# Where the outputs of a recurrent layer are computed: in the scans' slots or in the attention's gaps

## The chip, the core and the metric

The kernel runs on one core of a Trainium2 chip. The metric is the device time of one execution in microseconds: 1647.23 us is the median of three runs (1642.21 to 1647.71). Its engines are TensorE (PE in the profile; PEld is its loading of weights), VectorE (DVE), ScalarE (ACT), GpSimd (POOL) and SyncE (SP, which here only issues DMAs). SBUF is the memory on the chip that all of them work from, PSUM the one that TensorE writes to.

## What is computed

Eight batches of 512 tokens with 256 features go through four layers, each added to its input after a layernorm. All is fp32.

```python
x = x + _L0_attn_a_ref(_layernorm(x), ...)   # a: layernorm, Mamba mixer with a scan over the tokens, FFN 256-1024-256
x = x + _L0_ffn_ref(_layernorm(x), ...)      # b: a recurrence over the batches, then an output
x = x + _L0_attn_b_ref(_layernorm(x), ...)   # c: attention, 16 heads of 16 features
x = x + _L0_ffn_ref(_layernorm(x), ...)      # d: the same recurrence as b, same weights

# b and d: x is [8, 512, 256]; the recurrence runs over the 8 batches, all tokens side by side
def step(c, xt):
    ft = sigmoid(xt @ wf.T + c @ uf.T + bf)
    it = sigmoid(xt @ wi.T + c @ ui.T + bi)
    gt = tanh(xt @ wc.T + c @ uc.T + bc)
    return ft * c + it * gt
h = tanh(x @ wo.T + c_final @ uo.T + bo)     # every batch's output needs the state behind the last batch
```

So the output of layer b has two parts: a product x @ wo of each batch by itself, and a product of the final state, one for all batches, which is known only when the recurrence has gone through all eight.

## The kernel before

The work goes in three stages. The order of the instructions on PE, DVE and ACT is written out by hand, as short words in strings that name pieces of work; the order of POOL and SP is written out too in the first stage, and behind it is left to a scheduler.

**Stage 1, Mamba and recurrence b** (`mamba_and_recurrence`, L847). A batch's scan takes 16 slots, a line of text each (SLOTS, L789; LAST, L809, for the last batch; REST, L828, for what stands behind the last scan). Each slot scans two units of eight channels (`scan_pair`, L420: the scan at L424 and a product at L428, both on DVE), whose inputs SP loads from DRAM. In the slots stand pieces of other batches: of the next one its preparation (`i`, `e`), of the previous one the Mamba output and the FFN (`o`: projection L464, `up` L518, `down` L542), and recurrence b. Recurrence b of a batch begins in the next batch's slots (`r`) and ends in those of the one behind (`q`). `recurrent_step` (L615) makes its pieces: stats, norm, transposes (`turn`), and for each gate (f, i, g) and half m of the features a product with the inputs (`gate_inputs`, L595), one with the state (`gate_state`, L604) and a tanh (L610); `hold` and `update` (L677, L686, L687) make the new state on DVE. The pieces `output0` and `output1` (L691 to L702) multiply the transposed input by wo, a half of the tokens each, 8 matmul instructions of 128x256 in the profile; `output_` copies the sum from PSUM to SBUF (L707), and behind the second half the tile `pre` is stored to DRAM by a DMA that ACT issues (L710).

**Stage 2, attention c and recurrence d** (`attention`, L1239). A batch has 4 groups of 4 heads, and a group 4 rows of 128 tokens, which makes 16 rows. In each row the program goes: the scores of the next group for its maxima (`row_max`, L1084; PE at L1079 to the PSUM tag `two` with three buffers, DVE maximum L1090), the first gap of GAPS (L1191), the scores for the exponents (`attend`, L1109; the same tag, ACT exponent L1116), the second gap. The word `v` in a gap (`catch_up`, L1284) is the values' product of the row before (L1125), and in the rows 4, 8, 12 and 0 it ends a group: `collect` (L1134) copies the group's sum out on ACT (L1141) and SP issues eight DMAs of 32 KB, four to `o_c` and four to `sum_c` (L1146). `max` is the transposition of the maxima and their sum into the queries (L1101, L1106). The other words are pieces: `n` the preparation of the next batch, `d` and `e` recurrence d of the batch two behind and one behind, so that attention batches 0 and 1 have none of `d`; `c` and `o` the division by the sums (`divide{k}{half}`, L1155: reciprocal L1158 and product L1160 on DVE; k = 0 needs groups 0 and 1, k = 1 groups 2 and 3) and the output projection (L1166). Apart from `two`, gaps' products share one PSUM buffer, tag `one`.

The words `p` are what is left of layer b's output (`late_output`, L1211): load `pre` back from DRAM (L1218, one buffer), add the state's part `cu` (L1222), tanh (L1225), add to x (L1229). Batches 0 and 1 are done ahead of the rows, batches 2 to 7 in the gaps of attention batches 0 to 5, one each.

**Stage 3** (`stage_d_rest`, L1307) ends recurrence d and writes the outputs.

The function `part_of` (L119) gives the first half (".a"), the second (".b") or all of the tokens; `recurrent_step` and the FFN's pieces take such a half, and a gate of half the tokens keeps its PSUM in the tag `da` and its scratch in the scan's buffers (`hc`, L668 to L671).

Of the kernel before, what the change touches and what calls it, by code (L numbers as in the profile page):

```python
# [15 lines left out]
P = 128  # L16
B = 8
L = 512
# [596 lines left out]
def recurrent_step(cx, d, b, tok, tok_tag, ch, ch_tag, t=None, half=None):  # L615
# [27 lines left out]

    def turn_(k):
        nc.scalar.copy(t.xT[:, k, tk], ps_of["turn", k][:, tk])
        if k == KC - 1 and d.keep:
            d.xT[b] = cx.xdram.tile([P, KC, L], F32, tag=f"xT{b}", name=f"xT_dram_{n}")
            nc.sync.dma_start(d.xT[b], t.xT)

    def inputs(g, m):  # L650
        ps_of[g, m] = gate_inputs(cx, n, g, m, t.xT, fill(), tk)
# [27 lines left out]
    def update(m):  # L679
# [8 lines left out]
        if m == KC - 1 and half != 0:  # L688
            d.s = t.s

    def output(i):  # L691

        ps_of["output", i] = ps = cx.psum.tile([P, 2, E], F32, tag=fill(), name=f"ps_o_{n}_{i}")
        for j in range(2):
            for k in range(KC):
                nc.tensor.matmul(
                    ps[:, j, :],
                    t.xT[:, k, ts(2 * i + j, P)],
                    cx.gw[:, WO, k, :],
                    start=(k == 0),  # L700
                    stop=(k == KC - 1),
                )  # L702
# [10 lines left out]
    for name, f in (  # L713
        ("turn{}", turn), ("turn{}_", turn_), ("hold{}", hold), ("update{}", update),
        ("output{}", output), ("output{}_", output_),
    ):
        for i in range(2):
            pieces[name.format(i)] = lambda f=f, i=i: f(i)
    for g in range(3):
        for m in range(KC):  # L720
            for what, f in (("", product), ("_", tanh), ("x", inputs), ("s", state), ("s_", tanh)):
# [104 lines left out]
""".strip().split("\n")  # L826

REST = """  # L828
y o.gate1 o.proj0 o.proj1 o.add_proj o.stats o.norm o.residual
o.turn0 o.turn0_ o.turn1 o.turn1_ o.up0 o.up0_ o.up1 o.up1_ o.up2 o.up2_ o.up3 o.up3_ o.down0  # L830
o.down1 o.add0 o.up4 o.up4_ o.up5 o.up5_ o.add1 o.up6 o.up6_ o.up7 o.up7_ o.down2 o.down3 o.add2
o.add3 r.stats r.norm r.turn0 r.turn0_ r.turn1 r.turn1_
r.f0 r.f0_ r.hold0 r.i0 r.i0_ r.g0 r.g0_ r.update0
r.f1 r.f1_ r.hold1 r.i1 r.i1_ r.output0 r.output0_ r.g1 r.g1_ r.update1 r.output1 r.output1_
""".strip().split("\n")

FRONT = """
# [9 lines left out]
def mamba_and_recurrence(cx, a, w, d):  # L847
# [3 lines left out]
    for b, t in enumerate(T):  # L851
        t.da, t.hc, t.bx, t.dl_rep, t.dx_rep, t.y, t.ps = {}, {}, {}, {}, {}, {}, {}
        i = mamba_in(cx, a, t, b)
        o = mamba_out(cx, a, t, b)
        r, shared = {}, Ctx()
        for half in (None,):
            r |= recurrent_step(cx, d, b, cx.tok, "h", cx.ch, ("T", 3), shared, half)
        for who, ahead, pieces in (
            ("e", 2, i), ("i", 1, i), ("a", 0, i), ("c", 0, o), ("o", -1, o), ("r", -1, r), ("q", -2, r),
        ):  # L860
            parts[who, b - ahead] = pieces

    def piece(b, one):
        who, what = one.split(".", 1)
        if (who, b) in parts:
            parts[who, b][what]()

    for one in FRONT.split():
# [320 lines left out]


GAPS = """  # L1191
d.turn0 v n.stats d.turn1 | d.f0x
v | -
v o.divide10 | d.f0s
v d.i0x d.i0s n.norm | max
v | o.divide11 o.project0
n.turn0 | p.load v
d.g0x d.g0s | v
v n.turn1 | n.queries0 max
v | p.sum o.project1  # L1200
d.update0 d.f1x e.stats | v
v d.f1s | n.vals1 n.queries1 p.tanh
v | max
d.i1x d.i1s c.divide01 | v
n.vals0 | c.divide00 v
v p.add e.norm | d.g1x
d.g1s d.update1 | max v
""".strip().split("\n")


def late_output(cx, cu, d, b):  # L1211

    nc = cx.nc
    t = Ctx()

    def load():
        t.pre = cx.att.tile([P, TC, E], F32, tag="pre", bufs=1, name=f"pre_back_{b}")
# [21 lines left out]
def attention(cx, c, d, d_b, cu):  # L1239
# [19 lines left out]
        for b in range(B)  # L1259
    }  # L1260
    for b in range(2, B):
        parts["p", b - 2] = late[b]
    for b in range(B):
        parts["n", b - 1] = attention_in(cx, c, b)
        parts["c", b] = parts["o", b + 1] = attention_out(cx, c, b)
# [24 lines left out]
    for at, (b, g) in enumerate(steps):  # L1290
        po = None
        for t in range(TC):
            if at + 1 < len(steps):
                b1, g1 = steps[at + 1]
                row_max(cx, c, b1, c.made[b1], g1, t)
            first_gap, second_gap = GAPS[g * TC + t].split("|")
            fill(b, g, first_gap)
            es = attend(cx, b, c.made[b], g, t)
            fill(b, g, second_gap)
# [207 lines left out]
```

## Time and profile before

| | |
|---|---|
| median of 3 runs | 1647.23 us |
| profiled execution | 1647.11 us, its span 1645.3 us |
| mean granted TensorE clock | 0.949 |
| scans, one batch, from the third on | some 86 us |
| from the last scan's gate to the first attention scores (749.98 to 849.84) | 99.9 us |
| attention batch 0, 1, a later one (first scores to first scores) | 77.5, 75.9, 92.0 us |
| output products of layer b (L696) | 128 matmul instructions, 0.215 us apart when nothing waits |
| load of pre (L1218), 8 of 512 KB | 3.2 to 3.6 us from issue to landing |

How to read it: the page gives busy time by engine; stretches give the same between two times, with the clock granted to TensorE; the timeline lists instructions in order of time, runs of one kind merged, with start, length, engine, line, output<-inputs and shape; brackets name what ended an idle time. The chain of waits is followed back from the last instruction to what released each step. A matmul's end is modelled, so its start and the next one's start say more than its length.

### The profile page before, as it was taken

How to read it: one execution, taken by the hardware profiler on the slowest of the kernel's cores; microseconds unless marked ns; L12 is line 12 of the kernel's file. 1: busy time of each engine (PE TensorE's matmuls, PEld its weight loads, DVE VectorE, ACT ScalarE, POOL GpSimd, SP SyncE). 2: the span in 40 equal slices, each digit the busy share in tenths (PEclk: the TensorE clock that was granted, in tenths of full speed). 3: DMA queues.
4: the chain of work that ended last, by engine and by line, in shares of the span. 5: the costliest groups of instructions: out<-in, count | busy, mean ns of one | idle time of the engine just before them, and what ended most of it. 6: DMA issues, size and time to landing. Idle time of an engine off the chain costs nothing.

```text
span 1645.3 us, 19612 instructions
## 1 busy us (share of the span) xinstructions
PE 1489.6 (91%) x6756; PEld 700.2 (43%) x6756; DVE 1171.5 (71%) x1649; ACT 890.8 (54%) x1332; POOL 529.9 (32%) x307
## 2 busy tenths in 40 slices
PE   4347889999999999898879999999999999999998
PEld 1103536465555545556532333333333333333346
DVE  3699998989899989951156777675675767656435
ACT  5775858585868675532214555454545445454522
POOL 2576767767675846623100000000000000000000
PEclk8656989999999999999988999999999999999999
DMA  6989897989989787920211111101010110100123
GB/s 207 246 205 249 202 245 182 270 197 259 229 234 251 218 237 197 240 71 13 67 52 33 31 28 39 26 21 34 20 42 15 39 26 27 26 11 23 30 93 128
DMA packets 110435, 196.02 MB, mean 119 GB/s; under 512 B 16480, under 2 KB 26016, under 8 KB 110336
## 3 DMA queue, kind: packets, MB, share of 16 engines
q1 hardware_dynamic: 107680, 186.61, 43.5%
q10 hardware_dynamic: 1824, 5.15, 0.9%
q0 software_dynamic: 832, 3.02, 0.5%
q8 instruction: 53, 0.87, 0.2%
q14 instruction: 46, 0.38, 0.1%
HBM read 159.06 MB, written 23.07 MB: 111 GB/s over the span
## 4 chain that ended last, share of the span: by engine, by line
PE 68%; DVE 18%; ACT 5%; DMA 4%; issue 3%; POOL 2%; SPq 0%; DVEq 0%; ACTq 0%; POOLq 0%
PE ps_s_c L1079 10%; PE ps_e_c L1079 9%; DVE hc_a L424 8%; PE ps_o_c L1125 8%; PE ps_f_o L518 6%; PE ps_f_o L542 5%; DMA dl_rep_a<-dl_dram_a 4%; DVE hc_a L428 4%; PE ps_v_c L1053 2%; PE ps_w_c L1166 2%; PE ps_f_d L595 2%; PE ps_i_d L595 2%; PE ps_f_d L604 2%; PE ps_g_d L595 2%; PE y_a L437 2%
## 5 line engine op out<-in xcount | busy, mean ns | idle before, releaser
L1090 DVE TENSOR_REDUCE mp<-ps_s_c 128x2 f32<-128x1024 f32 x256 | 301.9, 1221 | 182.9 <-PE ps_s_c L1079 182.5
L415 POOL TENSOR_TENSOR bx_a<-dx_rep_a,B_a 128x1024 f32<-128x1024 f32 x128 | 302.4, 2374 | 98.4 <-DVE hc_a L424 55.4
L1116 ACT ACTIVATE e_c<-ps_e_c 128x1024 f32<-128x1024 f32 x256 | 248.9, 1021 | 155.4 <-PE ps_e_c L1079 152.5
L424 DVE TENSOR_TENSOR_SCAN hc_a<-da_a,bx_a 128x512 f32<-128x512 f32 x256 | 298.5, 1205 | 5.7 <-ACT da_a L408 5.2
L408 ACT ACTIVATE da_a<-dl_rep_a,neg_a 128x512 f32<-128x512 f32 x256 | 173.4, 688 | 131.1 <-DVE hc_a L424 90.1
L1079 PE MATMUL ps_s_c<-keys,q_c 32*128 32x512 f32 x1024 | 184.3, 646 | 2.2 <-ACT e_c L1116 1.7
L1079 PE MATMUL ps_e_c<-q_c,keys 32*128 32x512 f32 x1024 | 169.1, 644 | 3.7 <-DVE mp L1090 3.7
L428 DVE TENSOR_TENSOR hc_a<-hc_a,Cp_a 128x512 f32<-128x512 f32 x256 | 161.0, 669 | 0.0
L1125 PE MATMUL ps_o_c<-e_c,va 128*32 128x512 f32 x1024 | 138.9, 608 | 0.4 <-ACT oT_c L1141 0.3
L518 PE MATMUL ps_f_o<-h_o,w 128*128 128x256 f32 x512 | 121.3, 387 | 0.5 <-ACT f_o L531 0.3
L84 POOL TENSOR_TENSOR rs_d<-ve_d,neg_half 128x4 f32<-128x4 f32 x8 | 8.1, 1015 | 342.5 <-DVE ve_d L83 342.5
L542 PE MATMUL ps_f_o<-w,f_o 128*128 128x256 f32 x512 | 114.2, 381 | 4.0 <-ACT f_o L531 4.0
L437 PE MATMUL y_a<-hc_a,sum 128*32 128x512 f32 x512 | 92.5, 701 | 23.9 <-DVE hc_a L428 15.5
L518 PEld LDWEIGHTS ps_f_o<-h_o,w 128*128 128x128 f32 x512 | 96.7, 192 | 35.6 <-issue 12.2
L542 PEld LDWEIGHTS ps_f_o<-w,f_o 128*128 128x128 f32 x512 | 96.4, 190 | 23.2 <-ACT f_o L531 5.6
L84 POOL TENSOR_TENSOR rs_c<-ve_c,neg_half 128x4 f32<-128x4 f32 x8 | 8.1, 1014 | 301.1 <-DVE ve_c L83 301.1
L1079 PEld LDWEIGHTS ps_s_c<-keys,q_c 32*128 32x128 f32 x1024 | 59.0, 185 | 100.0 <-issue 38.3
L1079 PEld LDWEIGHTS ps_e_c<-q_c,keys 32*128 32x128 f32 x1024 | 51.6, 185 | 101.2 <-issue 67.3
L531 ACT ACTIVATE f_o<-ps_f_o,vecs 128x256 f32<-128x256 f32 x128 | 52.5, 469 | 33.5 <-PE ps_f_o L518 30.7
L240 PE MATMUL ps_in_a<-hT_a,w_in 128*128 128x512 f32 x128 | 69.2, 679 | 1.1 <-ACT hT_a L235 1.1
L1125 PEld LDWEIGHTS ps_o_c<-e_c,va 128*32 128x32 f32 x1024 | 20.4, 108 | 92.4 <-issue 82.6
L552 DVE TENSOR_TENSOR x<-x,ps_f_o 128x256 f32<-128x256 f32 x32 | 13.4, 417 | 61.3 <-PE ps_f_o L542 61.0
(222 smaller groups left out, 2162.6 us busy)
## 6 DMA issues: line engine op xcount, KB each, us to landing
dl_rep_a<-dl_dram_a SPq DMA_DIRECT2D x256, 256.0 KB, 6.6
dx_rep_a<-dx_dram_a SPq DMA_DIRECT2D x256, 256.0 KB, 6.6
x<-in_x_dram SPq DMA_DIRECT2D x8, 512.0 KB, 9.4
pre_dram_b<-pre_b ACTq DMA_DIRECT2D x8, 512.0 KB, 5.0
pre_back<-pre_dram_b SPq DMA_DIRECT2D x8, 512.0 KB, 3.3
keys<-xT_c SPq DMA_DIRECT2D x128, 32.0 KB, 1.9
o_c<-oT_c SPq DMA_DIRECT2D x128, 32.0 KB, 1.9
sum_c<-oT_c SPq DMA_DIRECT2D x128, 32.0 KB, 1.9
```

The costliest lines, as they stand in the source:

```text
L408: cx.nc.scalar.activation(t.da[u], t.dl_rep[u // 2][:, u % 2, :], AF.Exp, scale=a.A[:, u : u + 1])
L415: cx.nc.gpsimd.tensor_mul(t.bx[pair], t.dx_rep[pair], t.B.unsqueeze(1).to_broadcast([P, 2, L]))
L424: cx.nc.vector.tensor_tensor_scan(t.hc[u], t.da[u], t.bx[pair][:, u % 2, :], 0.0, ALU.mult, ALU.add)
L428: cx.nc.vector.tensor_mul(t.hc[u], t.hc[u], t.Cp)
L437: cx.nc.tensor.matmul(t.y[k][head(j), :], a.sum[:, r, :], t.hc[4 * quad + j], start=(r == 0), stop=(r == QR - 1),)
L518: nc.tensor.matmul(ps[:, m, :], a.w1[:, k, ts(m0 + m, P)], t.h2[:, k, ts(half, L // 2)], start=(k == 0), stop=(k == KC - 1),)
L542: nc.tensor.matmul(ps, t.f[:, m, ts(c % 2, P)], a.w2[:, m, :], start=(m == 0), stop=(m == FC - 1),)
L595: cx.nc.tensor.matmul(ps[:, tk], cx.gw[:, g, k, ts(m, P)], xT[:, k, tk], start=(k == 0), stop=False)
L1079: cx.nc.tensor.matmul(ps[:, i, :], lhs[rows, :], rhs[rows, :], start=True, stop=True)
L1090: cx.nc.vector.tensor_reduce(c.mp[:, t, h : h + 2, DH], ps, AX.X, ALU.max, negate=True)
L1116: cx.nc.scalar.activation(e, ps, AF.Exp)
L1125: cx.nc.tensor.matmul(po[head(j), :], c.va[b % 2][:, t, g * HG + j, :], es[j // 2][:, j % 2, :], start=(t == 0), stop=(t == TC - 1),)
```

## The change

1. For batches 2 to 7 the pieces `output0`, `output1` and their copies no longer exist in stage 1 (words that stand in the strings for them are skipped). In their place the transposed input `xT` is stored to DRAM, by a DMA that ACT issues, when its transposes have been copied. Batches 0 and 1 keep the old way.
2. `late_output` of batches 2 to 7 loads `xT` back, makes the product with wo in two halves (PSUM tag `one`), adds `cu` from PSUM (DVE), and does the tanh and the sum into x by halves. These are the words `p`, `s` and `t`: three batches in each of attention batches 0 and 1, with a gap order of their own, GAPS_01.
3. GAPS, the order for the attention batches from 2 on, is written anew.
4. REST is written anew: the FFN, the norms and the transposes behind the last scan go by halves of the tokens, and so does recurrence b of the last batch.

```diff
@@ -643,9 +643,9 @@
 
     def turn_(k):
         nc.scalar.copy(t.xT[:, k, tk], ps_of["turn", k][:, tk])
-        if k == KC - 1 and d.keep:
-            d.xT[b] = cx.xdram.tile([P, KC, L], F32, tag=f"xT{b}", name=f"xT_dram_{n}")
-            nc.sync.dma_start(d.xT[b], t.xT)
+        if k == KC - 1 and half != 0 and later:
+            d.xT[b] = cx.xdram.tile([P, KC, L], F32, tag=f"xT_{d.name}{b}", name=f"xT_dram_{n}")
+            (nc.sync if d.keep else nc.scalar).dma_start(d.xT[b], t.xT)
 
     def inputs(g, m):
         ps_of[g, m] = gate_inputs(cx, n, g, m, t.xT, fill(), tk)
@@ -688,8 +688,10 @@
         if m == KC - 1 and half != 0:
             d.s = t.s
 
+
+    later = d.keep or b >= 2
+
     def output(i):
-
         ps_of["output", i] = ps = cx.psum.tile([P, 2, E], F32, tag=fill(), name=f"ps_o_{n}_{i}")
         for j in range(2):
             for k in range(KC):
@@ -715,7 +717,8 @@
         ("output{}", output), ("output{}_", output_),
     ):
         for i in range(2):
-            pieces[name.format(i)] = lambda f=f, i=i: f(i)
+            if not (later and name.startswith("output")):
+                pieces[name.format(i)] = lambda f=f, i=i: f(i)
     for g in range(3):
         for m in range(KC):
             for what, f in (("", product), ("_", tanh), ("x", inputs), ("s", state), ("s_", tanh)):
@@ -826,12 +829,12 @@
 """.strip().split("\n")
 
 REST = """
-y o.gate1 o.proj0 o.proj1 o.add_proj o.stats o.norm o.residual
-o.turn0 o.turn0_ o.turn1 o.turn1_ o.up0 o.up0_ o.up1 o.up1_ o.up2 o.up2_ o.up3 o.up3_ o.down0
-o.down1 o.add0 o.up4 o.up4_ o.up5 o.up5_ o.add1 o.up6 o.up6_ o.up7 o.up7_ o.down2 o.down3 o.add2
-o.add3 r.stats r.norm r.turn0 r.turn0_ r.turn1 r.turn1_
-r.f0 r.f0_ r.hold0 r.i0 r.i0_ r.g0 r.g0_ r.update0
-r.f1 r.f1_ r.hold1 r.i1 r.i1_ r.output0 r.output0_ r.g1 r.g1_ r.update1 r.output1 r.output1_
+y o.gate1 o.proj0 o.proj1 o.add_proj.a o.stats.a o.norm.a o.residual.a o.add_proj.b o.stats.b o.residual.b
+o.turn0.a o.turn1.a o.turn0_.a o.turn1_.a o.up0 o.up0_ o.up1 o.up1_ o.norm.b o.up2 o.up2_ o.up3 o.up3_ o.turn0.b o.turn1.b o.turn0_.b o.turn1_.b o.down0 o.down1 o.add0 o.add1
+r.stats.a o.up4 o.up4_ o.up5 o.up5_ r.norm.a o.up6 o.up6_ o.up7 o.up7_ r.turn0.a r.turn1.a r.turn0_.a r.turn1_.a o.down2 o.down3 r.f0.a r.f0_.a r.hold0.a o.add2 o.add3
+r.i0.a r.i0_.a r.stats.b r.g0.a r.g0_.a r.update0.a r.norm.b r.f1.a r.f1_.a r.hold1.a r.i1.a r.i1_.a r.turn0.b r.turn0_.b r.turn1.b r.turn1_.b r.g1.a r.g1_.a r.update1.a
+r.f0.b r.f0_.b r.hold0.b r.i0.b r.i0_.b r.g0.b r.g0_.b r.update0.b r.f1.b r.f1_.b r.hold1.b r.i1.b r.i1_.b r.g1.b r.g1_.b r.update1.b
+r.output0.a r.output0_.a r.output1.b r.output1_.b
 """.strip().split("\n")
 
 FRONT = """
@@ -853,7 +856,7 @@
         i = mamba_in(cx, a, t, b)
         o = mamba_out(cx, a, t, b)
         r, shared = {}, Ctx()
-        for half in (None,):
+        for half in (None, 0, 1) if b == B - 1 else (None,):
             r |= recurrent_step(cx, d, b, cx.tok, "h", cx.ch, ("T", 3), shared, half)
         for who, ahead, pieces in (
             ("e", 2, i), ("i", 1, i), ("a", 0, i), ("c", 0, o), ("o", -1, o), ("r", -1, r), ("q", -2, r),
@@ -862,7 +865,7 @@
 
     def piece(b, one):
         who, what = one.split(".", 1)
-        if (who, b) in parts:
+        if (who, b) in parts and what in parts[who, b]:
             parts[who, b][what]()
 
     for one in FRONT.split():
@@ -1189,22 +1192,42 @@
 
 
 GAPS = """
-d.turn0 v n.stats d.turn1 | d.f0x
-v | -
-v o.divide10 | d.f0s
-v d.i0x d.i0s n.norm | max
-v | o.divide11 o.project0
-n.turn0 | p.load v
-d.g0x d.g0s | v
-v n.turn1 | n.queries0 max
-v | p.sum o.project1
-d.update0 d.f1x e.stats | v
-v d.f1s | n.vals1 n.queries1 p.tanh
-v | max
-d.i1x d.i1s c.divide01 | v
-n.vals0 | c.divide00 v
-v p.add e.norm | d.g1x
-d.g1s d.update1 | max v
+d.turn0 v | n.stats d.turn1
+v | o.divide11 d.f0x
+d.f0s | v
+d.i0x d.i0s | v max
+d.g0x d.g0s | o.divide10 v
+o.project0 d.update0 | v
+n.norm o.project1 | v
+n.turn0 v | max
+d.f1x | v
+c.divide00 d.f1s | v
+n.turn1 v | n.vals0
+n.vals1 e.stats n.queries0 | max v e.norm
+d.i1x c.divide01 | v d.i1s
+d.g1x | v
+v | d.g1s
+v | max n.queries1 d.update1
+""".strip().split("\n")
+
+
+GAPS_01 = """
+p.load v n.stats p.out0 | -
+- | v o.divide10
+p.fin0 p.out1 | n.norm v
+n.turn0 p.fin1 v | max
+o.divide11 v | s.load s.out0
+v n.turn1 | -
+- | o.project1 v
+s.fin0 v | max
+s.out1 | v
+s.fin1 n.vals0 | v
+v o.project0 e.stats n.queries0 | -
+- | t.load max v c.divide01
+t.out0 | v n.queries1
+v t.fin0 | t.out1 e.norm
+v | n.vals1 c.divide00
+t.fin1 v | max
 """.strip().split("\n")
 
 
@@ -1212,6 +1235,36 @@
 
     nc = cx.nc
     t = Ctx()
+
+    def load_input():
+        t.xT = cx.att.tile([P, KC, L], F32, tag="pre", bufs=1, name=f"xT_back_b{b}")
+        nc.sync.dma_start(t.xT, d.xT[b])
+
+    def product(i):
+        ps = cx.psum.tile([P, 2, E], F32, tag=cx.fill, name=f"ps_o_b{b}_{i}")
+        for j in range(2):
+            for k in range(KC):
+                nc.tensor.matmul(
+                    ps[:, j, :],
+                    t.xT[:, k, ts(2 * i + j, P)],
+                    cx.gw[:, WO, k, :],
+                    start=(k == 0),
+                    stop=(k == KC - 1),
+                )
+        t.th = cx.att.tile([P, 2, E], F32, tag="th", bufs=1, name=f"th_b{b}_{i}")
+        nc.vector.tensor_add(t.th, ps, cu[:, 2 * i : 2 * i + 2, :])
+
+    def finish(i):
+        nc.scalar.activation(t.th, t.th, AF.Tanh)
+        x = cx.X[b][:, 2 * i : 2 * i + 2, :]
+        nc.vector.tensor_add(x, x, t.th)
+
+    if b in d.xT:
+        return {
+            "load": load_input,
+            "out0": lambda: product(0), "fin0": lambda: finish(0),
+            "out1": lambda: product(1), "fin1": lambda: finish(1),
+        }
 
     def load():
         t.pre = cx.att.tile([P, TC, E], F32, tag="pre", bufs=1, name=f"pre_back_{b}")
@@ -1259,7 +1312,7 @@
         for b in range(B)
     }
     for b in range(2, B):
-        parts["p", b - 2] = late[b]
+        parts["pst"[(b - 2) % 3], (b - 2) // 3] = late[b]
     for b in range(B):
         parts["n", b - 1] = attention_in(cx, c, b)
         parts["c", b] = parts["o", b + 1] = attention_out(cx, c, b)
@@ -1293,7 +1346,7 @@
             if at + 1 < len(steps):
                 b1, g1 = steps[at + 1]
                 row_max(cx, c, b1, c.made[b1], g1, t)
-            first_gap, second_gap = GAPS[g * TC + t].split("|")
+            first_gap, second_gap = (GAPS if b > 1 else GAPS_01)[g * TC + t].split("|")
             fill(b, g, first_gap)
             es = attend(cx, b, c.made[b], g, t)
             fill(b, g, second_gap)
```

## The prediction

> **What bounds the kernel now.** I read the page first, then busy time by stretches, then the chain of work that ended last, then TensorE's own timeline. All times are of the profiled execution: 1647.11 us, of which the span is 1645.3; the median of the three runs is 1647.23, so what I add to the one holds for the other.
>
> ```profile
> PE 1489.6 (91%) x6756; PEld 700.2 (43%) x6756; DVE 1171.5 (71%) x1649; ACT 890.8 (54%) x1332; POOL 529.9 (32%) x307
> ```
> ```profile
> 749.00:793.00 44.00, 37.03 (x160) 29.59 (x153) 6.71 (x19) 10.89 (x23) 15.47 (x18) 0.92 0.03 12
> 793.00:832.00 39.00, 32.41 (x92) 17.67 (x92) 7.89 (x21) 8.44 (x14) 6.27 (x8) 0.91 0.26 87
> 860.60:938.20 77.60, 74.41 (x429) 24.73 (x428) 53.20 (x58) 39.32 (x43) 3.38 (x2) 0.92 0.12 31
> 938.20:1014.00 75.80, 74.36 (x452) 26.32 (x448) 57.13 (x71) 40.76 (x47) 4.59 (x4) 1.00 0.11 29
> 1197.90:1289.80 91.90, 91.90 (x508) 33.64 (x504) 60.87 (x78) 45.51 (x56) 4.58 (x4) 1.00 0.11 29
> ```
> TensorE is the engine of the whole. The stretches (from:to, length, busy PE, PEld, DVE, ACT, POOL, clock) are the two halves of what stands behind the last scan, attention batches 0 and 1, and one later batch. Batches 0 and 1 take 77.6 and 75.8 us, the later ones 92: those carry the second recurrence. "91.90 of 91.90" is not full use: a matmul block that waits for a buffer is recorded longer.
>
> **The scans.** There the chain swaps between TensorE and VectorE once a batch; its TensorE part ends so:
>
> ```profile
> 538.23 3.65 PE ps_f_o L518 x16
> 541.88 1.73 PE ps_o_b L696 x8
> 543.61 3.47 PE ps_f_o L542 x16
> ```
> L696 is the first output half: on the path, 1.73 us. The second half runs while the chain is on VectorE, and the two PSUM copies (0.59 each) are on ScalarE beside it: both free. Outputs of batches 2 to 5 stand in scans 4 to 7: **4 x 1.73 = -6.9**. The xT store that takes the place of the pre store has its size (512 KB) and issuer (ScalarE, 0.33 us an issue); no row shows it, so bounds: 0, and +2.3 for the one scan that now holds both stores (512 KB at the 230 GB/s of that stretch). I take 0.
>
> **Behind the last scan.** (a) Two output halves (741.87 and 747.03, 3.44 us) leave TensorE's unbroken run. The gate at 749.98 follows on VectorE, where the state update (end 749.34) now hides under the second half; without it the update ends at 747.6 and is late next: -2.3. (b) Gate to first up matmul is 13.6 us (749.98 to 763.56), TensorE nearly idle. With half the tokens: two 0.69 gate steps, projection half 1.7, add 0.7, half the stats 1.5, POOL 1.3, two normalizations 1.1, transposes and copies 2.1, some 9.1 in all; POOL clears attention tiles in this stretch and delays the scales by 1.0 now, which I keep: 10.1, so -3.5. (c) First up to the end of the last gate is 61.6 (763.56 to 825.2). In halves TensorE need not stop: 32 up instructions 8.6 (cold, as now), the other 96 of up and down 20.7, twelve half gates at 1.72, three pairs of half transposes 0.6 each, 0.5 for changes: 52.2, so -9.4, of which 1.7 is an output and the rest the 8.4 us pause and the slow first gate after it (3.40 for 1.88). (d) Tail: half-size tanh and update end 1.55 behind the last gate, not 2.4, the state product follows closer, -1.3; VectorE's 0.9 wait for the reloaded pre goes, as no store ends just ahead of it, -0.9. Sum **-17.4**. Bounds: -19 without POOL's delay; -13 if the clearing of attention tiles waits for the half gates' scratch (they borrow scan buffers) and pushes POOL's 12 us in front of the first attention scales.
>
> **Waits inside an attention row.** A row is scores s (1.07), first gap, exponent scores e (1.07), second gap, with values v (1.00) in one of the gaps. Later batch, four blocks:
>
> ```profile
> 1205.19 1.07 PE L1125 MATMUL ps_o_c<-e_c,va 128*32 128x512 f32 x8
> 1206.19 1.52 PE L1079 MATMUL ps_e_c<-q_c,keys 32*128 32x512 f32 x8
> 1207.71 1.92 PE L1079 MATMUL ps_s_c<-keys,q_c 32*128 32x512 f32 x8
> 1209.56 1.06 PE L1125 MATMUL ps_o_c<-e_c,va 128*32 128x512 f32 x8
> ```
> With only v (1.00) ahead, e took 0.45 more; with nothing behind e, s took 0.78 more; elsewhere the transposed maxima alone (0.58) gave 0.64, v alone 0.23, 1.58 or more nothing. That fits two rules: e waits 1.45 less the first gap (less what s waited), s waits 1.24 less the second gap (less what e waited): three score buffers, VectorE frees the first after one 1.18 maximum, ScalarE after one 0.97 exponent. By these rules batch 1 comes to 76.4, measured 75.85; the waits of the 91.95 us batch are 4.86.
>
> **Batches 0 and 1.** The six moved batches bring 12 halves of 1.92: 11.5 a batch. In batch 1 the work without waits rises from 63.6 to 75.1; the waits fall from 12.3 to 8.8 (rules over the 16 new rows 7.95, plus 0.85 where VectorE's extra adds delay a transpose): **+8.0**. So the empty gaps hide only a third of it. Batch 0: its first output waits for a reload that can't be issued before late batch 1 has left the buffer (865.08); landing 3.3, so the half runs from 868.5. Rows 0 to 3 end 3.2 later than now (885.8 against 882.56), rows 4 to 15 take 59.7 against 55.6: **+7.3**. Later reloads need SP to issue them ahead of their place in the text, as it does now:
>
> ```profile
> 865.08 0.33 SPq L1218 DMA_DIRECT2D pre_back<-pre_dram_b  x1
> 886.01 2.40 SPq L1146 DMA_DIRECT2D o_c<-oT_c  x4
> ```
> The load is written a row behind this collect, and goes 21 us ahead of it. Freed from batches 2 to 5, the late adds and tanh (VectorE 2.4, ScalarE 1.05) gain nothing: the batch without them is as long.
>
> **Batches 2 to 7.** The new gap order has no empty gap: by the rules 3.7 us of waits for 4.86, -1.1 each. Against this, c.divide00 now stands in row 9's first gap, and the collect that it needs (group 1) in row 8's second gap. How long a collect behind e takes is seen in row 12 of now:
>
> ```profile
> 1271.41 1.14 PE L1079 MATMUL ps_e_c<-q_c,keys 32*128 32x512 f32 x8
> ...
> 1274.47 0.59 ACT L1141 COPY oT_c<-ps_o_c 128x512 f32<-128x512 f32 x1
> ...
> 1275.09 2.40 SPq L1146 DMA_DIRECT2D o_c<-oT_c  x4
> ...
> 1277.53 2.48 SPq L1146 DMA_DIRECT2D sum_c<-oT_c  x4
> ```
> Eight issues of some 0.6, one behind the other, the last 8.0 after e began, landing 1.9 (its minimum and median): data at 9.9. VectorE, in order, would be free at 5.9 (e 1.07, v 1.00, s 1.3, maxima); it stands 4.0, divides 2.17, and row 10's maxima queue behind it: the first ends at 13.3. Row 10's e, due at 10.3, needs that buffer: **+3.1**, and nothing later in the batch gives it back, as the rows behind have no waits to shorten. Net +2.0, six times **+12.0**. Bounds: 0 to 4 for the 3.1. The same question for divide11 in row 1 gives nothing: data at 7.0, 0.4 us ahead of row 2's scores.
>
> Here a rule of the Trainium skill speaks for a cheaper wait: "DMA: Bandwidth & Descriptors", section "Issuing engines are not separate DMA queues", calls the time to initiate a DMA usually small relative to the DMA itself. The rows differ: 4.9 us of issues, 1.9 of landing. By the rule the data would be there at 5.6, before VectorE asks, and the sum would be 1631.5. A second rule, "TensorE: Matmul & The Clock Gate", Part 1, says a window of some 3.4 us idle halves the clock; the 6 us wait in batch 0 would then cost, an estimate from that page, 1.7 more: 1651.8.
>
> **The sum.** -6.9 - 17.4 + 8.0 + 7.3 + 12.0 = +3.0: 1650.1 us, I say **1650**: the gains and what is paid for them nearly cancel.
>
> **Rivals.**
> - *The divide waits for nothing* (TensorE finds other buffers, or the transfers come sooner): -18.6, 1631, faster. For it: in today's order no divide waits. Against: today it stands four rows behind its collect.
> - *SP issues the reloads where they are written*, behind row 4's collect: slower. The load lands 9.0 us after the v that collects, TensorE is at the output after 1.1: 7.9 in each of batches 0 and 1, 1666. It decides from the point where the load is issued later than row 3. Against: the two SP rows above.
> - *The halves behind the last scan bring half* of (b) to (d), because POOL or a buffer ring of three orders them otherwise: +7.5, 1658.
> - *Further waits in the denser rows* of single-buffered PSUM ("one") in batches 0 to 7, 1 to 1.5 us a batch: +10, 1660.
>
> **Chances.** Forecast 0.50 (own range 1642 to 1658), first rival 0.18, second 0.10, third 0.11, fourth 0.11. 0.5% of the time is 8 us, about what a measurement of this kernel can tell from no change: below 1639 lie the first rival and 0.02 of the forecast, 0.20; above 1655.5 the other three and 0.04 of the forecast, 0.36; 0.44 between. The range takes in the first rival and the third and fourth, and leaves out the second and the far ends: 1631 to 1664.
>
> **What would show it.** Stretch from the last scan's end to the first attention score some 17 us shorter, no pause ahead of the last gates. Attention batches of 84 to 85 us twice, then 94. In each later batch one e block of 4 us (for 1.07) in row 10, and VectorE idle some 4 us ahead of a reciprocal, released by a sum_c transfer. Wrong if that wait isn't there, if the reload issues come behind collects, or if scans 4 to 7 don't shorten by 1.7 each.

## The result, and the profile after

The changed kernel takes 1696.66 us (median of 4 runs, 1694.78 to 1701.74), the kernel before 1646.17 on the same chip: ratio 1.0315, 95% interval 1.0284 to 1.0346. Forecast was 1650, with a range from 1631 to 1664. The change is slower by 50.5 us, and the prediction was wrong. The profiled execution after has 1694.78 us and a span of 1692.8 (before 1645.3).

The busy times, first part of the page after:

```profile
PE 1503.8 (89%) x6804; PEld 718.2 (42%) x6804; DVE 1175.1 (69%) x1671; ACT 885.3 (52%) x1336; POOL 530.6 (31%) x312
```

Nearly the same work as before (PE is recorded busy for 14 us more) in a span that is 47.5 us longer: most of what is new is waiting. Stretches after (from:to, length, busy PE, PEld, DVE, ACT, POOL, granted clock, DMA share, GB/s): last scan's end to the first `up` matmul, from there to the last gate's end, from there to the first attention score, attention batches 0 and 1, a later batch:

```profile
723.80:752.70 28.90, 24.45 (x77) 11.16 (x76) 10.77 (x24) 5.70 (x10) 2.79 (x4) 0.99 0.00 1
752.70:812.90 60.20, 55.20 (x236) 46.67 (x236) 7.99 (x26) 16.92 (x40) 8.25 (x13) 0.92 0.16 55
812.90:848.90 36.00, 17.04 (x52) 10.44 (x52) 9.22 (x25) 5.48 (x8) 15.37 (x17) 0.67 0.13 38
859.75:945.90 86.15, 79.63 (x473) 32.63 (x472) 57.55 (x67) 39.87 (x47) 3.38 (x2) 0.93 0.14 41
945.90:1030.05 84.15, 83.16 (x497) 34.49 (x496) 62.75 (x82) 42.59 (x53) 4.60 (x4) 1.00 0.12 32
1225.00:1322.40 97.40, 95.10 (x506) 34.88 (x504) 58.35 (x76) 44.49 (x55) 4.58 (x4) 0.96 0.09 22
```

The first three stretches took 36.0, 62.0 and 24.3 us before; the third of them, in the kernel before:

```profile
825.54:849.84 24.30, 15.79 (x61) 10.33 (x60) 9.62 (x24) 6.29 (x9) 3.39 (x2) 0.79 0.25 79
```

The way to the last gate became 8.8 us shorter, but the third stretch 11.7 longer, with PE busy for 17 of 36 us at a clock of 0.67 and POOL for 15. Laid beside the terms of the prediction (profiled spans, us):

| stage | forecast | after less before |
|---|---|---|
| scans, to the last scan's end (727.6, 723.8) | -6.9 | -3.8 |
| from there to the first attention score (122.2, 125.2) | -17.4 | +2.9 |
| attention batch 0, first scores to first scores (77.5, 86.2) | +7.3 | +8.7 |
| attention batch 1 (75.9, 84.2) | +8.0 | +8.3 |
| batches 2 to 7 and what follows | +12.0 | +31.4 |
| sum | +3.0 | +47.5 |

**Where a later batch loses.** TensorE around row 10 of one of them (start, length, line, output<-inputs, shape; in brackets the idle time ahead and what ended it):

```profile
1284.26 1.13 PE L1082 MATMUL ps_e_c<-q_c,keys 32*128 32x512 f32 x4
1287.69 1.87 PE L1082 MATMUL ps_e_c<-q_c,keys 32*128 32x512 f32 x4 [2.30 <-DVE mp L1093]
1289.49 3.78 PE L1056 MATMUL ps_v_c<-wv,xT_c 128*128 128x256 f32 x8
1293.20 1.89 PE L1082 MATMUL ps_s_c<-keys,q_c 32*128 32x512 f32 x8
```

and VectorE there:

```profile
1284.29 1.75 DVE L1161 RECIPROCAL sum_c<-sum_c 128x256 f32<-128x256 f32 x1 [4.66 <-DMA sum_c<-oT_c]
1286.07 0.42 DVE L1163 TENSOR_TENSOR o_c<-o_c,sum_c 128x256 f32<-128x256 f32 x1
1286.42 2.35 DVE L1093 TENSOR_REDUCE mp<-ps_s_c 128x2 f32<-128x1024 f32 x2
```

VectorE stands 4.66 us before the reciprocal that c.divide00 brings, the maxima of row 10 queue behind it, and the e block is stopped in its middle: 3.43 from its first half to its second, for 0.54. That is the wait which the prediction drew. What it did not have is the next rows: the second half of e takes 1.80 for 0.54, the values' projection 3.71 for 1.92, the next scores 1.82 for 1.07. No pause is recorded there. The granted clock of the 8 us behind the stop is 0.58:

```profile
1288.00:1296.00 8.00, 8.00 (x25) 3.92 (x22) 1.63 (x2) 1.61 (x2) 0.00 (x0) 0.58 0.05 12
```

**Where the halves' gain goes.** POOL's first clearing of attention tiles before:

```profile
750.14 1.80 POOL L967 MEMSET mp<- 128x2048 f32 x1 [26.94 <-PE y_a L437]
```

POOL behind the last scan, after:

```profile
793.15 1.51 POOL L953 TENSOR_SCALAR uo<-uo 128x512 f32<-128x512 f32 x1 [5.37 <-DMA uo<-in_uo_dram]
794.65 0.71 POOL L84 TENSOR_TENSOR rs_b7.b<-ve_b7.b,neg_half 128x2 f32<-128x2 f32 x1
...
814.59 1.80 POOL L970 MEMSET mp<- 128x2048 f32 x1 [18.95 <-DVE c_b7.a L687]
...
826.06 0.53 POOL L996 COPY wv_b_wide<-vecs 128x128 f32<-128x128 f32 x2
```

and TensorE:

```profile
796.32 0.96 PE L115 MATMUL ps_xT_b7.b<-ident,xn_b7.a 128*128 128x128 f32 x2 [4.09 <-ACT xn_b7.a L106]
...
814.63 1.97 PE L750 MATMUL ps_cu_b<-uo,c_b7.a 128*128 128x256 f32 x8 [1.74 <-DVE c_b7.a L687]
826.41 2.08 PE L997 MATMUL ps_out_bias<-ow,wv_b_wide 128*128 128x256 f32 x4 [9.82 <-POOL wv_b_wide L996]
829.00 3.78 PE L750 MATMUL ps_cu_b<-uo,c_b7.a 128*128 128x256 f32 x8 [0.51 <-DVE out_bias L998]
```

The halving of the weights uo (L953) waits 5.37 us for their transfer, the scales of the second half's norm stand behind it in POOL's order, and TensorE pauses 4.09 us for that half. The clearing of the attention tiles, which ran from 750 to 765 before, begins at 814.59, released by the last state update (L687): its memory is that of the scan's buffers, and the half gates keep their scratch there (e6 tests this). POOL then needs 12 us to `wv_b_wide`, out_bias waits for it, and the second half of the state product stands behind out_bias in TensorE's order.

### The profile page after: what moved, and what is told of

It reads as the page before. It is cut to its first block, busy times and chain, and to the rows that moved or that the text cites. A ratio compares the mean times of both kernels' runs of the same rounds, so it can differ in the third digit from the quotient of the medians.

```text
span 1692.8 us, 19749 instructions
## 1 busy us (share of the span) xinstructions
PE 1503.8 (89%) x6804; PEld 718.2 (42%) x6804; DVE 1175.1 (69%) x1671; ACT 885.3 (52%) x1336; POOL 530.6 (31%) x312
## 4 chain that ended last, share of the span: by engine, by line
PE 61%; DVE 20%; DMA 5%; ACT 5%; issue 4%; POOL 3%; SPq 2%; ACTq 0%; DVEq 0%; POOLq 0%
PE ps_e_c L1082 9%; PE ps_s_c L1082 9%; DVE hc_a L424 8%; PE ps_o_c L1128 7%; PE ps_f_o L518 4%; DVE hc_a L428 3%; PE ps_f_o L542 3%; DMA dl_rep_a<-dl_dram_a 3%; PE ps_v_c L1056 2%; PE ps_w_c L1169 2%; PE ps_f_d L595 2%; PE ps_g_d L595 2%; PE ps_i_d L595 2%; PE ps_g_d L604 2%; PE ps_i_d L604 2%
## 5 line engine op out<-in xcount | busy, mean ns | idle before, releaser
L1082 PE MATMUL ps_s_c<-keys,q_c 32*128 32x512 f32 x1024 | 179.7, 656 | 1.6 <-ACT e_c L1119 1.1
L542 PE MATMUL ps_f_o<-w,f_o 128*128 128x256 f32 x512 | 114.3, 381 | 3.6 <-ACT f_o L531 3.6
L437 PE MATMUL y_a<-hc_a,sum 128*32 128x512 f32 x512 | 91.9, 694 | 23.0 <-DVE hc_a L428 15.2
L518 PEld LDWEIGHTS ps_f_o<-h_o,w 128*128 128x128 f32 x512 | 96.8, 192 | 35.0 <-issue 12.0
L542 PEld LDWEIGHTS ps_f_o<-w,f_o 128*128 128x128 f32 x512 | 96.3, 190 | 22.8 <-ACT f_o L531 5.4
L1161 DVE RECIPROCAL sum_c<-sum_c 128x256 f32<-128x256 f32 x32 | 55.8, 1745 | 42.7 <-DMA sum_c<-oT_c 42.7
```

Of the source, the lines that this page charges most:

```text
L437: cx.nc.tensor.matmul(t.y[k][head(j), :], a.sum[:, r, :], t.hc[4 * quad + j], start=(r == 0), stop=(r == QR - 1),)
L518: nc.tensor.matmul(ps[:, m, :], a.w1[:, k, ts(m0 + m, P)], t.h2[:, k, ts(half, L // 2)], start=(k == 0), stop=(k == KC - 1),)
L542: nc.tensor.matmul(ps, t.f[:, m, ts(c % 2, P)], a.w2[:, m, :], start=(m == 0), stop=(m == FC - 1),)
L1082: cx.nc.tensor.matmul(ps[:, i, :], lhs[rows, :], rhs[rows, :], start=True, stop=True)
```

## The experiments

Ratios are to the kernel before, with 95% intervals. The stages of all runs are those of the profiled execution; a batch goes from its first transposed maxima to the next batch's, and "later" is the median of batches 2 to 6. A profiled execution is not the median one: that of e4 took 1657.64, 8 us above its median, the others lie within 3 us of theirs. The kernels e5 and e9 are made from the kernel before and leave the products of four batches out of the result; all others are made from the changed kernel. A diff shows the lines that matter, with "..." for lines left out.

| kernel | us | ratio | last scan's end | from there to first score | batch 0 | batch 1 | later |
|---|---|---|---|---|---|---|---|
| before | 1646.17 | 1 | 727.6 | 122.2 | 78.7 | 75.8 | 91.9 |
| changed | 1696.66 | 1.0315 (1.0284 to 1.0346) | 723.8 | 125.2 | 87.4 | 84.1 | 96.8 |
| e1 (divide later) | 1663.25 | 1.0098 (1.0083 to 1.0113) | 727.9 | 123.7 | 88.9 | 84.7 | 90.9 |
| e2 (old gaps, late batches) | 1669.19 | 1.0131 (1.0115 to 1.0146) | 731.5 | 124.5 | 87.4 | 84.0 | 91.9 |
| e3 (outputs only) | 1658.45 | 1.0066 (1.0049 to 1.0083) | 729.9 | 118.5 | 87.4 | 82.8 | 91.9 |
| e4 (halves only) | 1649.70 | 1.0028 (1.0013 to 1.0042) | 729.8 | 127.3 | 81.3 | 75.9 | 91.9 |
| e5 (scans only) | 1650.75 | 1.0025 (1.0011 to 1.0038) | 729.2 | 124.4 | 78.9 | 75.9 | 91.9 |
| e6 (scratch apart) | 1686.69 | 1.0256 (1.0240 to 1.0271) | 729.2 | 112.3 | 87.2 | 84.1 | 95.8 |
| e7 (e1 and e6) | 1649.89 | 1.0032 (1.0017 to 1.0047) | 728.3 | 110.8 | 87.1 | 84.4 | 90.9 |
| e8 (halves and gap order) | 1641.89 | 0.9976 (0.9964 to 0.9987) | 725.0 | 117.8 | 83.8 | 75.9 | 90.9 |
| e9 (e5 with filler) | 1643.43 | 0.9988 (0.9975 to 1.0000) | 723.5 | 122.0 | 77.7 | 75.9 | 91.9 |
| e10 (e8, two outputs moved) | 1639.41 | 0.9956 (0.9941 to 0.9972) | 727.4 | 113.7 | 81.9 | 79.0 | 90.9 |
| e11 (e10, uo not on POOL) | 1630.97 | 0.9899 (0.9882 to 0.9917) | 727.6 | 105.5 | 81.5 | 79.0 | 90.9 |

The changed kernel, e1, e2, e3, e6 and e7 run the same instructions up to the last scan's end, and that end lies between 723.8 and 731.5: a profiled scan stage alone tells nothing below some 8 us. The kernel before gave 1646.8 to 1647.6 beside e1 to e11.

**e1, the divide four rows later.**

```diff
-c.divide00 d.f1s | v
+d.f1s | v
...
-d.g1x | v
+d.g1x c.divide00 | v
```

> The changed kernel with one word moved: in attention batches 2 to 7 c.divide00 stands in row 13's first gap, four rows behind the v that collects its group, not in row 9's. Everything else is the change. My theory: the divide in row 9 waits for the last of eight transfers, VectorE holds row 10's maxima behind it, TensorE stops some 4 us and then runs slowly for some matmuls; together about 5 us in each of six batches. So 1697 - 6 x 5 = 1667 us (1660 to 1672), later batches of 91 to 92 us, the 42.7 us of VectorE idle ahead of L1161 gone, row 10's e block 1.1 to 1.6 us instead of 5.2. Rival 1, the new order of the words as a whole is too dense for the single buffer they share: 1690 or more, batches of 95 or more. Between, 1672 to 1688: both.

Measured 1663.25. A later batch:

```profile
1305.00:1396.00 91.00, 91.00 (x507) 33.55 (x505) 58.59 (x76) 44.57 (x55) 4.58 (x4) 1.00 0.09 24
```

PE without a pause and the clock at 1.00. Row 10's e block takes 1.08 to the next start, the values' projection behind it 1.92 (the batch before this one):

```profile
1274.38 1.14 PE L1082 MATMUL ps_e_c<-q_c,keys 32*128 32x512 f32 x8
1275.46 2.00 PE L1056 MATMUL ps_v_c<-wv,xT_c 128*128 128x256 f32 x8
```

One word was worth 33.4 us. VectorE's idle time ahead of the reciprocals falls from 42.7 us in the whole run to 13.7, not to nothing as expected: the six waits of 4.5 to 5.6 us at c.divide00 are gone, seven of some 1.9 us at another division, in the second row of a batch, are in both runs and don't stop TensorE.

**e2, the gap words of before in batches 2 to 7.** The change is the text of GAPS alone.

> The changed kernel with the gap words of the kernel before in attention batches 2 to 7 (the words of the late adds name nothing there any more); batches 0 and 1 and all ahead of them as changed. Both theories expect batches of 92.0 us again, so 6 x 4.9 less, 1667 us (1663 to 1672). What tells them apart is this run beside the one with only the divide moved: my theory has that one equal or up to 6 us faster than this one (the new order without the divide's wait saves 1.1 us a batch by the two wait rules), rival 1 has it 25 us slower.

Measured 1669.19, batches of 91.9. So rival 1 falls: the dense order is not too dense, it is 5.9 us better than the old one (e1 against e2; forecast 6 x 1.1 = 6.6).

**e3, only the outputs moved.**

```diff
-        for half in (None, 0, 1) if b == B - 1 else (None,):
+        for half in (None,):
```

and REST and GAPS (from batch 2 on) as before.

> The outputs of six batches moved as in the change, with the new gap words in batches 0 and 1, but the words behind the last scan whole, not in halves, and the old gap words in batches 2 to 7. My theory: against the kernel before, -3.7 from the scans, -2.3 for the two output halves of batch 6 at the last scan's end, -1.7 for the first half of batch 7's at the recurrence's end, -0.9 for the reload, and +8.7 and +8.3 in batches 0 and 1 (the last two as the changed kernel shows them): +8.4, 1654.6 us (1650 to 1659), later batches 92.0. Rival, the moved outputs cost something else too (stores of xT in the scans, reloads, buffers): 1660 or more. Rival, the outputs alone bring no loss and the halves do: 1647 or less.

Measured 1658.45, within the range given. The stretch behind the last scan is 3.7 shorter (the three terms for the outputs there add up to 4.9), and batches 0 and 1 are 8.7 and 7.0 longer.

**e4, only the halves.**

```diff
-    later = d.keep or b >= 2
+    later = d.keep
```

with all of GAPS and the late adds as before.

> Only the halves behind the last scan; all outputs stay in the scans' slots and behind the last scan, gap words as before. My theory: the last gate ends some 9 us earlier than before, but POOL clears the attention tiles only when the half gates' scratch is released, so that keys, the bias and the first attention score come within 2 us of before: 1645 us (1641 to 1649), with POOL's first clearing at 810 or later. Rival 2, the halves bring their gain where the outputs are not moved (the loss in the changed kernel lies elsewhere): 1637 or less. Rival 3, the halves lose by themselves (twice as many instructions, a colder clock): 1650 or more.

Measured 1649.70, ratio 1.0028: 0.7 above the range. In the profiled execution it is 5.1 longer than before from the last scan's end to the first score, and POOL's first clearing starts at 822.71; that execution is the longest of the kernel's ten, so only part of the 5.1 may belong to the median, which is 3.5 above before. So the halves with this scratch lose 2 to 7 us (the interval); my theory had them level, with the clearing as the reason. Rival 2 falls; rival 3, that halves lose by themselves, isn't excluded by this run, but by e6 and e8, where the same halves with scratch of their own are ahead.

**e5, only the scans.**

```diff
+        if k == KC - 1 and not d.keep and 2 <= b <= 5:
+            d.pre[b] = cx.xdram.tile([P, KC, L], F32, tag=f"pre{b}", name=f"pre_dram_{n}")
+            nc.scalar.dma_start(d.pre[b], t.xT)
...
-            pieces[name.format(i)] = lambda f=f, i=i: f(i)
+            if d.keep or not 2 <= b <= 5 or not name.startswith("output"):
+                pieces[name.format(i)] = lambda f=f, i=i: f(i)
```

> The kernel before, with the output products and copies of batches 2 to 5 left out of scans 4 to 7 and the xT stored in place of pre, by the same queue. The reloaded xT stands for pre in the late adds of those batches, so the products of four batches are missing from the computation; everything behind the last scan is as before. The prediction's term was 4 x 1.73 = 6.9 us: 1640 us (1638 to 1642), last scan ending 7 us earlier. Rival, the next chain (ScalarE and VectorE through the soft-plus and the stores) stands close behind TensorE's, and less than half is gained: 1644 to 1647.

Measured 1650.75, ratio 1.0025: TensorE does 64 matmul instructions less in the scans, and the kernel is slower. The rival is nearer, but falls too, since it had no loss. Two views bear on it. First, VectorE in the kernel before, where the prediction's chain steps from PE to DVE (the down product L542 at 543.61 for 3.47):

```profile
545.81 1.25 DVE L428 TENSOR_TENSOR hc_a<-hc_a,Cp_a 128x512 f32<-128x512 f32 x2
547.10 0.42 DVE L552 TENSOR_TENSOR x<-x,ps_f_o 128x256 f32<-128x256 f32 x1
547.44 2.33 DVE L424 TENSOR_TENSOR_SCAN hc_a<-da_a,bx_a 128x512 f32<-128x512 f32 x2
```

The add that takes the product has no idle time in front of it: VectorE's own work ends at 547.06, the product, whose end is modelled, at 547.08. The chain of waits had to name one of two that end within 0.02 us. Second, TensorE in e5, some us later:

```profile
556.00 2.81 PE L115 MATMUL ps_xT_b<-ident,xn_b 128*128 128x128 f32 x8 [2.60 <-ACT xn_b L106]
558.63 3.78 PE L595 MATMUL ps_f_b<-xT_b,gw 128*128 128x512 f32 x4
```

Here the second output half (1.73) used to fill the time until the normalized input comes. Without it TensorE pauses 2.60 and the f gate's four matmuls take 3.58 to the next start for 2.07. Stretches of 10 us from 550 and from 560, e5:

```profile
550.00:560.00 10.00, 7.34 (x18) 3.38 (x17) 9.93 (x22) 5.65 (x10) 7.33 (x6) 0.80 0.96 262
560.00:570.00 10.00, 10.00 (x32) 3.23 (x31) 9.49 (x11) 3.82 (x6) 9.28 (x5) 0.86 0.97 268
```

and before:

```profile
550.00:560.00 10.00, 9.29 (x37) 4.47 (x35) 9.93 (x21) 5.96 (x11) 7.20 (x6) 1.00 0.91 247
560.00:570.00 10.00, 10.00 (x34) 3.48 (x34) 10.00 (x15) 5.10 (x10) 10.00 (x6) 1.00 0.98 302
```

The clock falls from 1.00 to 0.80 and 0.86, and VectorE, which runs the scan, waits 0.51 for the gate at 565.11. It stands so at this gate in one of the three scans only, so the views show where time is lost, but not all of the 4 us that the kernel loses. In the three scans from 464 us on, that matmul has a median of 644 or 645 ns in every kernel with both output halves in the scans (before, e4, e8, e10, e11) and of 986 to 1062 ns in every one without either (changed, e1, e2, e3, e5, e6, e7).

**e6, the half gates' scratch apart.**

```diff
-        if half is None:
-            return cx.tmp.tile([P, L], F32, tag=what, name=f"{what}{m}_{n}")
-
-        return cx.scan.tile([P, L], F32, tag="hc", bufs=HC, name=f"{what}{m}_{n}")[:, tk]
+        return cx.tmp.tile([P, L], F32, tag=what, name=f"{what}{m}_{n}")[:, tk]
```

> The changed kernel with the half gates' scratch in its own two tiles, not in the scan's buffers; everything else as changed, the divide's wait too. My theory: POOL clears the attention tiles ahead of the last gates again, as in the kernel before; that sets the first normalization behind the last scan some 4 us later (7 us of clearing stand ahead of its scales), but out_bias no longer waits for POOL. From the last scan's end to the first attention score 125 less 8 (5 to 12 less), so 1697 - 8 = 1689 us (1685 to 1692). Rival, something else is late behind the last gate (reloads, the scaling of uo): 1693 or more.

Measured 1686.69, 10.0 less than the changed kernel, and POOL clears early again:

```profile
749.15 1.80 POOL L967 MEMSET mp<- 128x2048 f32 x1 [24.36 <-PE y_a L437]
...
756.23 0.70 POOL L84 TENSOR_TENSOR rs_o7.a<-ve_o7.a,neg_half 128x2 f32<-128x2 f32 x1
```

The scales of the first half now come behind 7 us of clearing (756.23, or 27.0 behind the last scan's end, for 25.8), 1.2 later, which is less than the 4 us I gave it. From the last scan to the first score: 112.3, 9.9 shorter than before.

**e7, both mended** (e1 and e6 together).

> The changed kernel with both: c.divide00 in row 13 and the half gates' scratch in its own tiles. My theory: the two add up, 1663 - 8 = 1655 us (1651 to 1659): what is left against the kernel before is the 16 us of the moved outputs in batches 0 and 1, less what the halves and the gap order then bring. Rival as for the scratch alone: 1660 or more.

Measured 1649.89, a little better than the range: alone the two bring 33.4 and 10.0, together 46.8. Mended so, the change still doesn't pay: batches 0 and 1 stay 8.4 and 8.6 us longer than before.

**e8, the outputs stay; halves and gap order mended.** In batches 2 to 7 the words of the late adds go into the new rows, batches 0 and 1 have the old ones:

```diff
-    later = d.keep or b >= 2
+    later = d.keep
...
-o.project0 d.update0 | v
+o.project0 d.update0 | p.load v
...
-d.f1x | v
+d.f1x | v p.sum
...
-n.turn1 v | n.vals0
+n.turn1 v | n.vals0 p.tanh
...
-v | d.g1s
+v p.add | d.g1s
```

> The outputs stay where the kernel before has them (scans' slots, and late adds in batches 0 to 3); halves behind the last scan with scratch of their own; in batches 0 and 1 the gap words of before, in batches 2 to 7 the new ones with c.divide00 in row 13 and the words of the late adds put into rows 5, 8, 10 and 14. My theory: the halves alone gave 1649.7, 8 less for the scratch, and 6 x 1.1 less for the gap order: 1635 us (1630 to 1640), faster than before. Rival, the halves can't pay (POOL's clearing delays their start as much as it delayed their end): 1641 or more.

Measured 1641.89, 0.24% faster than before, but 2 us above my range, and inside the rival's. The rival's reason doesn't hold, though: from the last scan's end to the first score the kernel is 4.4 us shorter than before, and the later batches are 1.0 shorter each. Most of what is missing is in batch 0, 83.8 us for 78.7. Its stretch up to 883.3:

```profile
851.80:883.30 31.50, 29.18 (x107) 8.74 (x105) 17.61 (x28) 8.92 (x9) 3.37 (x2) 0.52 0.06 17
```

PE is recorded busy for 29 of 31.5 us and stays at half its clock. In the kernel before, 24 us from the same point had 0.72. Why the clock comes up later here the runs don't show.

**e9, a filler in the scans.**

```diff
-            if d.keep or not 2 <= b <= 5 or not name.startswith("output"):
+            if d.keep or not 2 <= b <= 5 or not name.startswith("output") or (i == 1 and name == "output{}"):
```

> The run with the outputs of batches 2 to 5 left out of the scans, with one thing put back: the matmuls of each second output half (8 of 1.73 us together) run where they stood, and nothing reads their result. First halves and copies stay out, the reloaded xT still stands for pre. My theory now: that second half only filled a pause of TensorE behind the state gates of one step and ahead of the transposes of the next; without it the pause was 2.6 us, the granted clock 0.80 and 0.86 in the two stretches of 10 us, the f gate's input matmuls had a median of 1060 ns for 644, and VectorE waited for the gate. With it back: 644 again in all scans, last scan beginning at 722 to 727, and, as VectorE has no idle time there for the first half to give back, the time of the kernel before: 1646.5 us (1645 to 1648). The prediction's reading of the chain gives 1640, since only the first half was on it. Rival, the stores of xT cost the time: 1650 again.

The lines are those of e5 and of e9. Measured 1643.43, 7.3 less than e5 (6 by the ratios, whose intervals don't meet): matmuls whose result nobody reads make the kernel faster. It rules out that the xT stores cost the time, as they are still there. But my picture was too simple. The f gate's median is 644 in the first of the three scans and 1061 in the other two:

```profile
550.00:560.00 10.00, 8.40 (x26) 4.40 (x25) 9.93 (x22) 4.95 (x9) 7.97 (x5) 0.89 0.93 245
560.00:570.00 10.00, 10.00 (x33) 3.38 (x33) 9.70 (x15) 5.73 (x11) 9.60 (x6) 0.94 1.05 282
```

With a longest pause of 0.87 us left there (the stretches are in the second scan), the clock still falls, but less, and VectorE's gate update no longer waits (0.51 in e5). How the 7.3 divide among the scans, the traces don't settle, since the scan stage varies by that much from run to run. Against before, taking out the first halves is worth 0 to 4 us (the interval), not 6.9.

**e10, only the outputs of the last two batches moved,** on top of e8:

```diff
-    later = d.keep
+    later = d.keep or b >= 6
...
-d.turn0 v n.stats d.turn1 | d.f0x
-v | -
-v o.divide10 | d.f0s
-v d.i0x d.i0s n.norm | max
-v | o.divide11 o.project0
+s.load v n.stats | -
+v | s.out0
+v o.divide10 s.fin0 | -
+v s.out1 n.norm | max
+v s.fin1 | o.divide11 o.project0
```

> The mended halves and gap order (outputs in the scans, 1641.9), but the outputs of the last two batches, 6 and 7, which stand behind the last scan, moved into rows 0 to 4 of attention batches 0 and 1. My theory: behind the last scan 117.8 becomes 111 as in the kernel with both mended, so -7; each of the two batches gains 3.84 us of matmuls, a third to a half of it hidden, so +2 to +3 each, less what batch 0 gains if the products keep TensorE's clock up there (its first rows ran with e and s at 1.87 for 1.07 in the last run, 5 us in all). 1639 us (1633 to 1643). Rival, the outputs cost batches 0 and 1 their full length: 1643 or more.

Measured 1639.41, within the range. Against e8 it is 4.1 shorter behind the last scan (7 forecast), 3.1 longer in batch 1 and 1.9 shorter in batch 0, where the clock over the stretch shown for e8 is 0.76 instead of 0.52.

**e11, the scaling of uo away from POOL,** on top of e10:

```diff
-    nc.gpsimd.tensor_scalar_mul(cx.uo, cx.uo, 0.5)
...
-        nc.vector.tensor_add(
+        nc.vector.scalar_tensor_tensor(
             cu[:, 2 * i : 2 * i + 2, :],
             ps_c,
+            0.5,
             cx.rows["bo"].unsqueeze(1).to_broadcast([P, 2, E]),
+            ALU.mult,
+            ALU.add,
         )
```

> The kernel with the outputs of two batches moved, with the halving of uo taken from POOL and done in VectorE's add that follows the state product (one instruction for the one that was there). In the halves runs POOL's scaling of uo stood ahead of the second half's normalization and waited for its transfer: the scales came 6 us after their variance, TensorE paused 3.7 and its gates ran at 1.91 for 1.03. Without it: 4 us less (2 to 6) than the run beside it, 1635 us. Rival, VectorE or ScalarE is as late there: less than 1.5 us.

Measured 1630.97, 8.4 less than e10, more than expected, and 1.0% faster than before. POOL in e10:

```profile
798.90 1.51 POOL L950 TENSOR_SCALAR uo<-uo 128x512 f32<-128x512 f32 x1 [6.35 <-DMA uo<-in_uo_dram]
800.39 0.71 POOL L84 TENSOR_TENSOR rs_b7.b<-ve_b7.b,neg_half 128x2 f32<-128x2 f32 x1
```

and in e11:

```profile
793.05 0.71 POOL L84 TENSOR_TENSOR rs_b7.b<-ve_b7.b,neg_half 128x2 f32<-128x2 f32 x1 [0.75 <-DVE ve_b7.b L83]
```

The scales come when their variance is there; in e10 they came at 800.39, behind the scaling, which had waited 6.35 us for uo. TensorE's pause of 4.71 there is gone, and with it the gates at 1.91 for 1.03.

## Why the prediction was wrong, step by step

- **Batches 0 and 1**: right (15.3 forecast, 17.0 measured). The reload that SP was to issue early was issued at 864.19, the first output began at 867.84 (forecast 868.5), so the second rival falls. Its block took 3.68 us for 1.92, behind a pause of 6.00: an excess of 1.8, at a granted clock of 0.50. The Trainium skill's "TensorE: Matmul & The Clock Gate", Part 1, from which I had estimated 1.7 as a side remark and left out of the sum, agrees in size. That the pause did it isn't shown: the clock was at 0.50 ahead of it too (the scores at 859.75 took 2.09 for 1.07).
- **The gap order of batches 2 to 7**: right, 1.0 less a batch (91.9 to 90.9 in e1) for 1.1 forecast. The fourth rival (more waits in the shared buffer) falls with it for these batches.
- **c.divide00 in row 9**: the mechanism was right, to within 0.4 us. Data 10.3 behind the start of row 8's e block (forecast 9.9), row 10's e due at 10.2 (10.3), its buffer free at 13.6 (13.3); so the first rival, a divide that waits for nothing, falls. **The step that failed is the price, "+3.1, and nothing later in the batch gives it back": it costs 5.9 a batch** (96.8 against 90.9; e1 takes it away), since a stop of 2.9 us is followed by matmuls at a clock of 0.58: in the batch shown the values' projection and the next scores take 2.5 us more than in e1. Six times 2.8 is 17 us of the error. I had weighed a slower clock behind batch 0's pause, not behind this one. The skill's same page, "TensorE: Matmul & The Clock Gate", section "HAM oscillation — how this bites in real kernels", describes such a loop, in which each round's wait makes the next matmuls slow again; it gives pauses of over some 3.4 us as the danger, while here the clock fell behind 2.30 us of recorded idle time.
- **Behind the last scan**: the working of (a) to (c), -15.2 to the last gate, was right for a kernel in which POOL isn't in the way: e11 needs 82.5 from the last scan's end to the last gate's end, 15.5 less than before, and 16.7 less to the first score (forecast -17.4). (The pieces listed under (b) add up to 9.8, not 9.1, so that term should have read -2.8.) **The step that failed is the bound "-13 if the clearing of attention tiles waits for the half gates' scratch".** I had named the cause and priced it at 4.4; it was 10 to 13 (e6 against the changed kernel, e7 against e1), since out_bias and half of the state product stand behind the clearing too, not only the attention's scales. **The second step is "In halves TensorE need not stop" in (c)**: the scaling of uo stands ahead of the second half's scales on POOL, TensorE stops 4.09 us, and its next gates run at 1.91 for 1.03. I had no term for it; taking it away is worth 8.4 (e11 against e10). Together the two take more than the term: +2.9 instead of -17.4, 20 us of the error.
- **Scans**: the step "L696 is the first output half: on the path, 1.73 us" failed. It was read from the chain of waits alone; VectorE's timeline shows no idle time at that step, and without the first halves 0 to 4 us were gained (e9), not 6.9. The second halves, which I had called free, filled a pause: without them too the kernel is slower than before (e5). The -3.8 of the table is within what that stage varies by.
- **The skill's rule on DMA issue** that I weighed and set aside is decided against by the run too: row 10 does wait for the transfers. "DMA: Bandwidth & Descriptors", "Issuing engines are not separate DMA queues", calls the issue time usually small; here the eight issues take 4.9 of the 10.3 us.

The rival that the halves bring half was on the right side, but not large enough: in the changed kernel the term is +2.9. By the table, the price of the wait, what stands behind the last scan and the scans (17, 20 and 3) make some 40 of the 44.5 us by which the spans miss the sum.

## What to carry to other kernels

Before you count a step of the chain of waits as a gain, look at the idle time of the instruction that takes over: where it has none, two chains end together, and removing one of them gives nothing. Price a stop of TensorE by its length and by the slow matmuls behind it, and ask of each matmul that you take away whether it was filling a pause. When work is cut into halves to close pauses, look at the engine that is in nobody's way (here POOL): which of its instructions stand ahead of each half, and whose memory the scratch of the halves holds.

## What the runs showed of the hardware

- TensorE's granted clock fell behind recorded pauses of 2 to 3 us: 0.57 to 0.79 over the next 8 us behind each of the six pauses of 2.17 to 3.26 us in row 10 of the changed kernel, 0.80 and 0.86 in the 10-us stretches around and behind the 2.60 of e5; the f gate's matmuls there took 1060 ns for 644. No length at which it falls is shown: in e9 it came to 0.89 with pauses of at most 0.87 us, and in the kernel before it stayed at 1.00 behind one of 2.20 (ended at 693.24).
- The clock can stay low while TensorE is recorded busy: 0.52 over 31.5 us with 29.2 us busy (e8, batch 0). What ends the state isn't shown.
- Matmuls without a reader can shorten a kernel: e9 is 7.3 us faster than e5, by 32 such instructions (8 in each of four batches).
